# Two masked attentions with their experts: VectorE in program order, the side work cut finer and moved apart, one gate product per bank, GpSimd for the sums

## The chip, the cores and the metric

The kernel runs on one core of one Trainium2 chip. The metric is the device time of one execution in microseconds. The kernel before takes 2669.72 us, the median of three runs (2664.33 to 2672.69). One further execution was profiled; its own time is 2684.83 us.

The engines of the core are TensorE (PE; its weight loads are listed as PEld), VectorE (DVE), ScalarE (ACT), GpSimd (POOL) and SyncE (SP). Each takes its instructions from a queue of its own, in the order in which they were put there, and waits for the others by semaphores.

## The reference, cut to what matters

The reference is a stack of four transformer layers on x of 4 sequences x 512 positions x 128 features, all in fp32. Every layer is a "macaron": half a feed-forward part, an attention, half the same feed-forward part again, each on the layer-normed x. The change concerns layer 1, whose feed-forward part holds a masked attention of its own and a mixture of experts, and which the kernel therefore runs twice:

```python
q = (q_in @ Wq.T + bq).reshape(B, S, H, D)   # q_in: x, rotated in pairs (cosine and sine)
scores = jnp.einsum('bqhd,bkhd->bhqk', q, k) * scale        # 16 heads of 8, causal
attn = jax.nn.softmax(jnp.where(causal, scores, -jnp.inf), axis=-1)
x1 = _layer_norm(x + attn_out, ln1_w, ln1_b)
gates = jax.nn.softmax(x1 @ gate_w.T + gate_b, axis=-1)     # 8 experts
_, top_idx = jax.lax.top_k(gates, 2)
expert_outputs = jnp.einsum('bsd,efd->bsef', x1, expert_w) + expert_b
moe_out = jnp.sum(sel * top_gates[..., None], axis=2)       # the two chosen ones
return _layer_norm(x1 + moe_out, ln2_w, ln2_b)
```

The kernel multiplies all eight experts and gives the six that were not chosen a gate of zero.

## The kernel before, in words

**Tiles.** A sequence of 512 positions is four tiles of 128. Positions lie on the partitions in `x` and `y` (128 x 16 tiles x 128 features), features lie on the partitions in `yT`.

**The masked attention** is `dense_attention` (L820), called by `l1_ffn` (L999) with `masked=True`, once as "l1f" and once as "l1g". It has 16 units, 4 sequences b times 4 head groups j, and each unit has four steps n, one for every tile of keys. A step has two halves. In a half, TensorE multiplies two blocks of scores by keys (`pk_at`, for the step itself) and two blocks of scores by queries (`pq_at`, for the step five later, `LEAD`). VectorE takes the maxima of the latter (`maxima`, L856: one instruction at L866 that adds the mask and reduces, into `nm`), ScalarE takes the exponentials of the former into `PT` (L894), GpSimd zeroes the triangle above the diagonal (the causal select, L897), and TensorE multiplies the weights of the step before with the values into `po_at` (`with_values`, L902). At the start of a unit the maxima are transposed and added to the queries (`qx`, L876); at its end the sums are transposed and divided (L939, L940).

**The PSUM banks** of this stage are three for `pk_at`, three for `pq_at` (tag "q"), one for `po_at` and one for the side work (tag "m"). The expert products take banks of tag "q".

**The side work.** The next sequence is prepared by a list of parts, each with a place relative to the first step of that sequence (`prepare`, L1007: norm, scale, transposes, rotation, queries, keys with their masked copies, values). A place of -17.5 is the second half of the 18th step before. When a sequence has finished its attention, `l1_experts` (L1056) puts its rest into a chain: `spare(gap, part, products)` appends a part that runs `gap` ticks after the one before, and `tick` (L307), called once in every half step, runs what is due. Of the parts that put products on TensorE (`products` true, the default) one at most runs in a tick. The chain, with its gaps:

```python
spare(2, statistics_of_y, False); spare(4, lambda: affine(1), False); spare(4, lambda: turn(b))
spare(2, gates); spare(2, choice, False); spare(3, turn_gates); spare(2, biases)
for t in range(TB): spare(2, lambda t=t: both(t))
spare(1, statistics_of_y, False); spare(4, lambda: affine(2), False); spare(2, residual, False)
leave_normed(b, spare, 2)     # statistics of x 1 tick later, scale 1, transposes 2
```

The statistics of `y` and of `x` are four pairs of instructions (L242, L245) and a root, whose power runs on GpSimd (L214, L215). `affine` scales with four ScalarE instructions (L279) and multiplies and adds on GpSimd (L1069, L1070). `residual` adds `y` to `x` on GpSimd (L1140), and `leave_normed` (L314) then norms the new `x` for the next stage (statistics, scale L257, transposes). `both(t)` multiplies one tile with all eight experts into two banks and adds the eight results, each times its gate, to `y` with eight VectorE instructions (`sum_up`, L1117), every one reading what the one before wrote. The last sequence, b = 3, does all this after the attention, and its elementwise work on VectorE.

**The order of the queues.** TensorE's instructions are kept in program order by `mm_in_order`, ScalarE's by `by_order` within the attention. VectorE's and GpSimd's instructions are put into their queues by the scheduler of the tile framework, in the order in which its own model of the run finds them ready.

## Time and profile before

| what | us |
|---|---|
| median of three runs | 2669.72 |
| the profiled execution, its own time | 2684.83 |
| its span, from the first to the last instruction | 2683.0 |
| first masked attention, starts of units 0 to 15 | 383.7 to 644.8 |
| second masked attention, starts of units 0 to 15 | 833.3 to 1091.7 |
| a causal select on GpSimd (L897), mean | 0.410 |
| an addition of 128x512 on GpSimd (L1070), mean | 1.27 |
| an addition of 128x128 on GpSimd (L1275), mean | 0.454 |
| one expert's gate product and sum on VectorE (L1117), mean | 0.348 |
| a 128x512 product out of PSUM on VectorE (L1025), mean | 0.687 |

The page of the profile gives busy times of the engines, the chain of work that ended last, and groups of instructions by line. PE's busy time includes the modelled ends of its pipelined products, so a busy PE may still be a waiting one; the length of a unit says more. The granted clock is TensorE's, as a share of its full speed. In a row of a group or a timeline, "out<-in" names the tiles, and what stands in brackets or after the bar is the idle time of the engine just before it and what released it. In the timeline a row may merge several instructions (x8).

### The profile page before, as it was taken

How to read it: one execution, taken by the hardware profiler on the slowest of the kernel's cores; microseconds unless marked ns; L12 is line 12 of the kernel's file. 1: busy time of each engine (PE TensorE's matmuls, PEld its weight loads, DVE VectorE, ACT ScalarE, POOL GpSimd, SP SyncE). 2: the span in 40 equal slices, each digit the busy share in tenths (PEclk: the TensorE clock that was granted, in tenths of full speed). 3: DMA queues.
4: the chain of work that ended last, by engine and by line, in shares of the span. 5: the costliest groups of instructions: out<-in, count | busy, mean ns of one | idle time of the engine just before them, and what ended most of it. 6: DMA issues, size and time to landing. Idle time of an engine off the chain costs nothing.

```text
span 2683.0 us, 50819 instructions
## 1 busy us (share of the span) xinstructions
PE 2274.4 (85%) x19070; PEld 1288.0 (48%) x19070; DVE 1776.3 (66%) x4790; ACT 1306.2 (49%) x3159; POOL 951.7 (35%) x1532
## 2 busy tenths in 40 slices
PE   6578589988679989988787778998899998799988
PEld 2255244443344434477567645555433333555555
DVE  3745667775676777565554488777567775877774
ACT  3056125443333544343443357776525554677773
POOL 2023023232232233214331377766310001876761
PEclk8789799998889999789778879999989999899998
DMA  3052000000000000246145701010000000110100
GB/s 146 8 175 73 0 1 2 1 1 1 1 1 1 1 5 1 84 146 216 32 139 160 246 23 23 21 23 19 1 1 1 1 1 9 27 23 19 23 21 13
DMA packets 40142, 113.21 MB, mean 42 GB/s; under 512 B 7064, under 2 KB 16536, under 8 KB 39384
## 3 DMA queue, kind: packets, MB, share of 16 engines
q1 hardware_dynamic: 36520, 100.94, 11.8%
q0 software_dynamic: 2944, 6.04, 1.1%
q8 instruction: 151, 2.47, 0.4%
q10 hardware_dynamic: 432, 2.98, 0.3%
q14 instruction: 95, 0.78, 0.1%
HBM read 79.78 MB, written 15.47 MB: 35 GB/s over the span
## 4 chain that ended last, share of the span: by engine, by line
PE 56%; DVE 21%; ACT 8%; POOL 8%; issue 5%; DMA 1%; another core or an unknown queue 0%; POOLq 0%; DVEq 0%; SPq 0%; ACTq 0%
PE pk_at L185 10%; PE po_at L185 6%; PE pa L185 4%; PE pq_at L185 4%; PE pag L185 4%; PE po L185 3%; ACT s L1737 3%; PE pg L185 2%; PE pe L185 2%; PE p_qk L185 2%; DVE t L1794 2%; DVE t L1791 2%; PE pz L185 2%; PE idle L185 2%; PE pt L182 2%
## 5 line engine op out<-in xcount | busy, mean ns | idle before, releaser
L894 ACT ACTIVATE PT<-pk_at 128x512 f32<-128x512 f32 (+3 forms) x768 | 335.3, 488 | 401.2 <-PE pq_at L185 254.0
L185 PE MATMUL pk_at<-qx,km 32*128 32x512 f32 (+3 forms) x1536 | 401.4, 555 | 5.9 <-ACT PT L894 2.7
L866 DVE CUSTOM_DVE_ANT_0 s<-pq_at,cst 128x384 f32<-128x384 f32 (+3 forms) x512 | 249.9, 488 | 99.0 <-PE pq_at L185 44.8
L185 PE MATMUL pq_at<-km,qT 32*128 32x128 f32 (+3 forms) x1024 | 275.8, 504 | 18.3 <-DVE nm L866 14.4
L1737 ACT ACTIVATE s<-s,nm,rn 128x128 f32<-128x128 f32 x512 | 245.5, 482 | 3.2 <-DVE nm L1849 3.0
L897 POOL TENSOR_SCALAR_AFFINE_SELECT PT<-PT 128x256 f32<-128x256 f32 x256 | 104.5, 410 | 381.7 <-ACT PT L894 381.6
L185 PEld LDWEIGHTS pk_at<-qx,km 32*128 32x128 f32 x1536 | 147.1, 190 | 154.3 <-issue 93.5
L185 PE MATMUL po_at<-PT,vh 128*32 128x128 f32 (+3 forms) x2432 | 205.6, 395 | 8.7 <-POOL PT L897 6.9
L868 DVE TENSOR_REDUCE nm<-pq_at 128x1 f32<-128x512 f32 x256 | 165.4, 685 | 55.3 <-PE pq_at L185 53.8
L1798 POOL TENSOR_TENSOR t<-t,t 128x1024 f32<-128x1024 f32 x64 | 151.2, 2362 | 109.7 <-DVE t L1794 105.1
L215 POOL TENSOR_TENSOR ln_r<-ir,minus_half 128x4 f32<-128x4 f32 x60 | 62.0, 1034 | 351.5 <-DVE ir L214 349.5
L185 PE MATMUL pq_at<-km,t 32*128 32x512 f32 x512 | 170.9, 661 | 0.7 <-DVE nm L868 0.4
L185 PE MATMUL p_qk<-w,hT 128*128 128x512 f32 x256 | 142.4, 684 | 15.6 <-DVE t L1794 9.6
L1861 POOL TENSOR_TENSOR s<-s,sm 128x1024 f32<-128x1024 f32 x64 | 121.3, 1896 | 52.1 <-DVE sm L1860 44.1
L185 PEld LDWEIGHTS po_at<-PT,vh 128*32 128x32 f32 x2432 | 54.4, 109 | 174.4 <-issue 128.5
L182 PE MATMUL pt<-ident,s 128*128 128x128 f32 x640 | 94.0, 295 | 48.5 <-POOL s L1861 32.0
L185 PEld LDWEIGHTS pq_at<-km,qT 32*128 32x128 f32 x1024 | 110.6, 191 | 48.9 <-DVE nm L866 28.9
L1419 POOL DMA_INDIRECT xg<-yd,come x60 | 57.5, 958 | 180.3 <-PE pt_x L182 72.3
L289 ACT COPY yT<-pt_y 128x512 f32<-128x512 f32 x56 | 32.7, 584 | 180.0 <-PE pt_y L182 179.5
L1737 ACT ACTIVATE sq<-p_qk 128x1024 f32<-128x1024 f32 x64 | 65.5, 1023 | 109.8 <-PE p_qk L185 61.6
L182 PEld LDWEIGHTS pt<-ident,s 128*128 128x128 f32 x640 | 79.0, 151 | 81.1 <-POOL s L1861 44.2
L1791 DVE TENSOR_TENSOR t<-p_qk,w 128x1024 f32<-128x1024 f32 x64 | 78.3, 1223 | 58.5 <-ACT sq L1737 53.0
(457 smaller groups left out, 5374.7 us busy)
## 6 DMA issues: line engine op xcount, KB each, us to landing
wf<-in_w2f_dram SPq DMA_DIRECT2D x45, 836.0 KB
vb<-v SPq DMA_DIRECT2D x112, 128.0 KB
w<-in_w2f_dram SPq DMA_DIRECT2D x15, 836.0 KB
skew<-qe SPq DMA_DIRECT2D x16, 512.0 KB
rel<-skew SPq DMA_DIRECT2D x64, 128.0 KB
od<-o SPq DMA_DIRECT2D x60, 64.0 KB
w<-in_w_dram SPq DMA_DIRECT2D x1, 3200.0 KB
w<-in_w_dram SPq DMA_DIRECT2D x12, 173.0 KB
```

Source lines behind the costliest of these rows:

```text
L182: return nc.tensor.transpose(dst, src, ident[: src.shape[0], : src.shape[0]])
L185: tc.keep_in_program_order(nc.tensor.matmul(dst, lhsT=lhsT, rhs=rhs, start=start, stop=stop))
L215: nc.gpsimd.tensor_tensor(dst, v, minus_half[:, :n], ALU.pow)
L866: nc.vector.tensor_tensor_reduce(s[:, :nk], pq[:, :nk], causal[:, S - nk :], 1.0, -BIG, ALU.add, ALU.max, to)
L868: nc.vector.tensor_reduce(to, pq, AX.X, ALU.max)
L894: by_order(nc.scalar.activation(PT[:, i, q0:], pk[:, q0:], AF.Exp, scale=SC8))
L897: nc.gpsimd.affine_select(d, d, pattern=[[0, 2], [1, P]], base=0, channel_multiplier=-1, compare_op=ALU.is_ge, fill=0.0)
L1419: nc.gpsimd.indirect_dma_start(xT[s], None, yds[k][:, :], bass.IndirectOffsetOnAxis(ap=come[:, i : i + 1], axis=0))
L1737: tc.keep_in_program_order(nc.scalar.activation(*args, **kw))
L1791: nc.vector.tensor_mul(by_head(t1), by_head(p3), over(tab[:, 0]))
L1798: nc.gpsimd.tensor_add(t1, t1, t2)
L1861: nc.gpsimd.tensor_mul(s, s, bcast(sm, P))
```

## The change

1. **VectorE in program order.** Every VectorE instruction now goes through a small wrapper that keeps it in program order while a flag is set. The flag is set in a masked attention from step 0 to its end. (The diff replaces `nc.vector` by `vector` everywhere; those lines are left out here.)
2. **Finer parts, further apart.** For the sequences 0 to 2 the chain of `l1_experts` is written anew. Statistics come in two halves, the means, the scaling and the affine steps in parts of their own, the choice of experts in four parts, and the gaps are larger. In `prepare`, for the sequences 1 to 3, the statistics are halved, the cosines and the output bias become parts of their own ahead of the rotation, and the masked copies of the keys come two at a time. The copy of the keys `kT` now shares the buffer of `qin`.
3. **One gate product per bank.** `gated` multiplies one tile with four experts into one bank, and one VectorE instruction multiplies that bank with the four gates into a tile `by_act` of 128 x 4 x 128, of which there are three buffers.
4. **GpSimd sums.** `summed` adds the two halves of a tile, 128x512, then 128x256, then 128x128, and adds the result to `y`, four GpSimd instructions.

Sequence 3 keeps the chain of before. Counted in ticks from the start of a chain, its parts lie as follows:

| part | before | after, sequence 0 | after, 1 and 2 | after, 1 in the second attention |
|---|---|---|---|---|
| statistics of y | 2 | 1, 2 | 1, 2 | 1, 2 |
| gate logits | 12 | 12 | 12 | 12 |
| expert tiles | 21, 23, 25, 27 | 21 to 35, a bank every 2 | 20 to 27, a bank each | 19 to 22, a tile each |
| residual | 34 | 46 | 38 | 32 |
| statistics of x | 35 | 49, 50 | 41, 42 | 34, 35 |
| scale, transposes | 36, 38 | 52, 54 | 44, 46 | 37, 39 |

```diff
+    class InOrder:
+        def __getattr__(self, name):
+            op = getattr(nc.vector, name)
+            def issue(*args, **kw):
+                i = op(*args, **kw)
+                if ordered["dve"]:
+                    tc.keep_in_program_order(i)
+                return i
+            return issue
+    vector = InOrder()
...
+    def statistics_in_parts(src, b):
...
+            for t in (2 * i, 2 * i + 1):
+                vector.bn_stats(st[:, t, :], src[:, b * TB + t, :])
+                vector.bn_aggr(mv[:, t, :], st[:, t, :])
+            if i:
+                inverse_root(keep, r, mv[:, :, 1], "ir4", ALU.add, 1e-5, nc.gpsimd)
...
+        if pinned == "parts":
+            spare(start, halves[0], False)
+            spare(1, halves[1], False)
+            spare(2, scale, False)
...
         for n in range(-LEAD, n_steps + 5):
+            ordered["dve"] = masked and n >= 0
...
                 def rotate():
-                    nc.vector.tensor_mul(seq["in"], pw, ST)
-                    nc.gpsimd.tensor_add(yb, yb, rows(VEC(vec, "1f_bo"), TB))
-                    nc.gpsimd.tensor_mul(t2, yT[:, b, :], CT)
+                    vector.tensor_mul(t2, pw, ST)
                     vector.tensor_add(seq["in"], seq["in"], t2)
...
+                        (-19, norm), (-18.5, norm_more), (-17, scale), (-15.5, features), (-13.5, cosines), (-12.5, biased),
+                        (-11.5, rotate), (-9.5, queries), (-7.5, keys), (-6.5, lambda: mark((0, 1))),
+                        (-6, lambda: mark((2, 3))), (-5.5, last),
...
+        def gated(t, half):
+            pe = two_banks("pe1")[0] if "d" in psum["bufs"] else bank("e" if "e" in psum["bufs"] else "q", "pe1")
+            mm_in_order(pe, yT[:, b, ts(t, P)], ew[:, ts(half, 512)])
+            st["by", t, half] = sb.tile([P, 4, D], F32, tag="by_act", name="by_act", bufs=3)
+            vector.tensor_mul(
+                st["by", t, half], pe.rearrange("p (e d) -> p e d", d=D), bcast(st["g"][:, t, 4 * half : 4 * half + 4], D)
+            )
+        def summed(t):
+            v, w = st.pop(("by", t, 0)), st.pop(("by", t, 1))
+            yt = y[:, b * TB + t, :]
+            nc.gpsimd.tensor_add(v, v, w)
+            nc.gpsimd.tensor_add(v[:, 0:2, :], v[:, 0:2, :], v[:, 2:4, :])
+            nc.gpsimd.tensor_add(v[:, 0, :], v[:, 0, :], v[:, 1, :])
+            nc.gpsimd.tensor_add(yt, yt, v[:, 0, :])
...
+        next_part = 0 if routed and b == 1 else 1
+        if b < B - 1:
+            normed_in_parts(1, 1)
+            spare(3, lambda: turn(b))
+            spare(2, gates)
+            for f, gap in ((grow, 1), (share, 1), (best, next_part), (two_best, 1)):
+                spare(gap, f, False)
+            spare(1, turn_gates)
+            spare(2, biases)
+            for t in range(TB):
+                for half in range(2):
+                    spare((next_part if half else 1) if b else 2, lambda t=t, half=half: gated(t, half), False)
+                    if t and half == 0:
+                        spare(0, lambda t=t: summed(t - 1), False)
+            spare(1, lambda: summed(TB - 1), False)
+            normed_in_parts(2, 2 + next_part)
+            spare(1, residual, False)
+            leave_normed(b, spare, 2, "parts", 2 + next_part)
+            return
```

`normed_in_parts(n, gap)` places a norm of y in the chain: the two halves of the statistics, the means on GpSimd, the scaling on ScalarE in two halves, the multiplication and the addition of the affine step on GpSimd, at the gaps gap, 1, 1, 2, 1, 0 and 1.

## The prediction

> **What bounds the kernel now.** I read the page first (busy shares, then the shares of the chain that ended last), then a table of engine busy time with one row per unit of the two masked attentions, then the timeline and the chain of waits inside the worst units.
>
> ```profile
> span 2683.0 us, 50819 instructions
> PE 2274.4 (85%) x19070; PEld 1288.0 (48%) x19070; DVE 1776.3 (66%) x4790; ACT 1306.2 (49%) x3159; POOL 951.7 (35%) x1532
> ...
> PE 56%; DVE 21%; ACT 8%; POOL 8%; issue 5%; DMA 1%; another core or an unknown queue 0%; POOLq 0%; DVEq 0%; SPq 0%; ACTq 0%
> ```
>
> TensorE leads over the whole span, but that is an average. The change touches only the two masked attentions. Each has 16 units (4 sequences, 4 head groups), and a unit begins with its addition into `qx` (L876). The starts, read from the timeline, run from 383.7 to 644.8 us (units 0 to 14 of the first) and from 833.3 to 1091.7 us (the second). Rows for units 3, 8, 10 and 14 of the first; the columns are window, length, busy time of PE, PEld, DVE, ACT and POOL, granted clock, DMA:
>
> ```profile
> 424.70:436.90 12.20, 12.11 (x124) 6.23 (x124) 8.92 (x35) 6.59 (x17) 3.25 (x8) 1.00 0.01 2
> 500.60:519.50 18.90, 18.70 (x148) 8.60 (x152) 14.62 (x53) 7.52 (x19) 4.46 (x9) 1.00 0.01 1
> 542.30:567.80 25.50, 19.69 (x150) 9.21 (x150) 15.27 (x67) 10.69 (x26) 9.57 (x15) 0.87 0.00 1
> 621.10:644.80 23.70, 19.66 (x134) 8.17 (x136) 12.83 (x50) 9.79 (x26) 10.39 (x15) 0.71 0.00 1
> sum 261.10, PE 242.31 PEld 109.56 DVE 186.40 ACT 119.91 POOL 81.67; mean PE 16.15 PEld 7.30 DVE 12.43 ACT 7.99 POOL 5.44
> ```
>
> Unit 3 has no side work: 12.2 us is what a unit costs by itself. Unit 8 carries 6.44 us of side products on TensorE (two expert tiles, biases, transposes) and takes 18.9: **0.3 us over** 12.2 + 6.44. Unit 10 carries 4.43 us (the timeline has keys 1.13, transposes 1.12, gate logits 1.03, values 1.16) and takes 25.5: **8.9 us over**, at a clock of 0.87. I worked this for every unit. By the busy tables of the side tiles these products sum to 48.6 us in the first attention and 49.1 in the second, so the floors are 15 x 12.2 + 48.6 = 231.6 and 232.1 us, against 261.1 and 258.4. **55.8 us** in all lie above the floors: 35.7 in units 10 and 14 (8.9, 8.7, 8.8, 9.3), 7.8 in unit 5 (5.1, 2.7), 10.7 in units 9 and 13, 1.6 elsewhere. The chain of waits of unit 10, in order of time, says why:
>
> ```profile
> 543.19 1.53 ACT y L279 x4
> 544.80 1.28 POOL y L1069
> 546.15 1.28 POOL y L1070
> 547.51 1.28 POOL x L1140
> 548.81 0.49 DVE ln_st L242 x2
> ...
> 551.00 1.05 POOL ln_r L215
> 552.07 0.78 DVE y L257 x2
> 552.85 0.60 DVE s L866
> 553.51 1.64 PE pq_at L185 x2
> ```
>
> and VectorE's own timeline:
>
> ```profile
> 544.90 0.08 DVE L866 DVE_READ_ACCUMULATOR2_ANT nm<- 128x1 f32 x1
> 548.81 0.49 DVE L242 BATCH_NORM_STATS2 ln_st<-x 128x6 f32<-128x128 f32 x2 [3.82 <-POOL x L1140]
> ```
>
> A statistics instruction that needs GpSimd's residual sits in VectorE's queue ahead of maxima whose scores are ready. VectorE idles 3.82 us, then 1.16 for GpSimd's power; TensorE runs out of score banks (it waits 1.93 and 2.38 us for `nm`) and then runs slower. Unit 5 of the first attention shows another form: eight statistics in one clump, four of them a later sequence's, which the program has some ten steps on. VectorE's queue is not in program order.
>
> **The change, part by part.** *VectorE in program order, parts further apart.* By the tick counts, the residual was tick 34 of a sequence's chain and the statistics tick 35; they become 46 and 49 (sequence 0), 38 and 41 (1 and 2), 32 and 34 (sequence 1 of the second attention). A tick is half a step, 12.2 / 8 = 1.5 us bare, so the residual gets about 3 to 5 us instead of 1.5, and it needs up to 3 x 1.27 of GpSimd. The cause of units 10 and 14 should go. I leave 2 us in each, since the affine still fills GpSimd there (in unit 14 `po_at` itself waited 1.58 + 0.95 us for a causal select): 35.7 - 8 = **27.7**. Of unit 5 I take two thirds (the clump is split and put back in its place), **5.2**; of units 9 and 13 half, **5.3**. Bounds: nothing, and all 55.8. No instruction is added by the order. What is late next in these units is TensorE itself.
>
> *One gate product per bank.* 24 tiles (three sequences, two attentions) lose eight L1117 of 0.35 us, 2.78, and gain two 128x512 products out of PSUM; L1025, of that size and source, takes 0.686, so 1.37. VectorE gets 1.41 x 24 = 34 us free, which is **not on the path**: the expert units 8 and 12 are only 0.3 and 1.7 (0.9 and 1.7) over their floors, so at most 4.6 us. TensorE's own two products a tile stay. I take nothing.
>
> *GpSimd sums.* Four additions a tile: 128x512 1.27 (L1070), twice 128x128 at 0.454 (L1275), 128x256 between these, by columns 0.73: 2.91 us a tile, 70 us in all. The causal selects (0.41, two a step) queue behind them, and `po_at` waits for those. In two half steps with a tile (2 x 1.53 + 2 x 1.12 = 5.3 us) GpSimd has 2.91 + 0.82 = 3.7, so it keeps up, but single selects come late. Bounds a tile: nothing, and 1.6 us, TensorE's longest wait for a select in the first attention. I take 0.3, near the lower end since the sum falls between selects: **-7**; ends 0 and -38.
>
> *A new wait.* `by_act` has three buffers, and the second product of a tile writes the first buffer of the tile before, so VectorE waits there for that tile's last addition, with the maxima behind it. Sequence 0 has 5.3 us between tiles, enough. For sequences 1 and 2 (12 such places) a sum begun at its tick ends after 2.91 + 0.41 = 3.3 us, a half step with one product is 2.65: 0 to 0.7 late, or 1.2 with both selects ahead. I take 0.25: **-3**; ends 0 and -14.
>
> [...] VectorE's instructions that read SBUF only are stretched by GpSimd, those out of PSUM not. Minimum, median and maximum, in ns:
>
> ```profile
> L214 DVE TENSOR_SCALAR ir<-ln_mv x48: 151/170/1279, 9.2 to 2270.1; 128x4 f32<-128x4 f32 x48
> L371 DVE TENSOR_TENSOR oh<-g,fm x16: 182/187/940, 484.1 to 1159.0; 128x32 f32<-128x32 f32 x16
> L1117 DVE SCALAR_TENSOR_TENSOR y<-pe,g,y x240: 300/351/353, 508.8 to 1173.9; 128x128 f32<-128x128 f32 x120
> ```
>
> The 1.28 us one began at 626.64, with a GpSimd addition that began at 626.63. The new products and the maxima read PSUM. Some ten small instructions may meet the new sums at up to 1.1 us; most of that is covered by VectorE's idle time. I take **-2**; ends 0 and -10. [...]
>
> *The tail.* Sequence 2's chain is 46 ticks to its last transpose instead of 38, so eight ticks of it move behind the attention. In the next stage TensorE already waits 5.40 us for this chain's L257 (at 685.75). I take 2 us each: **-4**; ends 0 and -10. Splitting keys, cosines and statistics moves instructions without adding any, but for 0.24 of GpSimd a norm. On SP's queue the store of y that a logits step issues in the second attention moves from tick 39 to 55, 40 and 47; the gathers need sequences 0 and 1, and for 1 it is one tick.
>
> Sum: 27.7 + 5.2 + 5.3 - 7 - 3 - 2 - 4 = **22.2 us** faster. The profiled execution took 2684.8 us (span 2683.0 and 1.8 around it), 15 more than the median 2669.7. I take the difference from the median: **2647 us**.
>
> **Rivals.** (A) The forecast, 2647, own range 2632 to 2662.
> (B) *Full cure:* the order also clears units 5, 9 and 13, and the sums fit between selects: 55.8 less 8 to 12 of costs is 46, so 2624. For it: units 1 to 4, with side work well spread, are at most 0.3 us over their floors. Against: GpSimd is fullest where the stalls are.
> (C) *The stall only moves:* VectorE now waits in strict order for GpSimd's sums and roots, and gives back what the residual cost: 38 less 36, so 2668. For it: every wait of the worst units ends on GpSimd. Against: the distances are doubled or tripled.
> (D) *Slower: GpSimd becomes the bound of the expert tiles.* Place: the select behind a sum. Price: 1.6 us x 24 = 38 and the buffer wait 14, against 38 cured; with 4 of tail it is 18 slower, 2688. It decides from about 1.2 us a tile on. For it: 2.91 us of GpSimd in a half step of 2.65, and in the second attention, sequence 1, a whole tile every half step. Against: units with 9 to 10 us of GpSimd stall by VectorE first.
>
> **Chances.** A 0.57, B 0.15, C 0.11, D 0.17. Faster by over 0.3% (8 us, about what a measurement can tell from no change) 0.72, within 0.11, slower 0.17. The range 2616 to 2684 leaves out the ends of B and D.
>
> **What would show it.** Right: units 10 and 14 near 15 to 19 us at a clock of 1.00; no `ln_st` wait for `x` L1140 above 0.5 us; 48 products out of PSUM near 0.69; POOL some 70 us busier; L1117 down to the last sequence's 48. Wrong: `po_at` waiting for the select over 1 us a tile (D), VectorE waiting for `by_act` or `ln_r` by several us (C). If units 8 and 12 fall below 18 us, the product was worth more than I gave it.

## The result, and the profile after

The kernel after takes 2685.16 us, the median of four runs (2678.21 to 2689.87), beside 2670.95 us for the kernel before in the same comparison: a ratio of 1.0056, with a 95% interval of 1.0036 to 1.0075. The forecast was 2647, a ratio of 0.9915. Two further comparisons on other chips (below) give 1.0007 (0.9992 to 1.0022) and 1.0026 (1.0009 to 1.0042). So the change is worth nothing to half a per cent of loss, where 0.8% of gain was forecast. The kernel before takes 2671 to 2687 us by chip; times are therefore compared within one batch only.

The page of the kernel after: its instructions by engine, and the shares of the chain that ended last.

```profile
PE 2272.7 (85%) x19070; PEld 1289.5 (48%) x19070; DVE 1753.4 (66%) x4637; ACT 1304.1 (49%) x3159; POOL 1022.4 (38%) x1637
...
PE 54%; DVE 21%; POOL 9%; ACT 8%; issue 5%; DMA 3%; SPq 0%; POOLq 0%; DVEq 0%; ACTq 0%
```

The parts went in at their forecast prices: GpSimd is 70.7 us busier (forecast 70), VectorE has 153 instructions fewer. The instructions of the new tile, with their count and their least, median and longest duration in ns:

```profile
L184 DVE TENSOR_TENSOR by_act<-pe,g x48: 681/691/693, 510.1 to 1142.5; 128x512 f32<-128x512 f32 x48
L1230 POOL TENSOR_TENSOR by_act<-by_act x24: 1262/1272/1282, 515.0 to 1143.2; 128x512 f32<-128x512 f32 x24
```

(Every VectorE instruction of the kernel after is recorded at L184, the helper's line; matmuls are at L200, transposes at L197.)

Now the units of the first attention, as in the prediction. An attention's units are counted from 0, and the floor of a unit is the prediction's: 12.2 us and the busy time of its side products. Rows of the kernel after for units 7, 10, 11 and 14: window, length, busy time of PE, PEld, DVE, ACT and POOL, granted clock, DMA.

```profile
482.60:501.20 18.60, 16.04 (x136) 7.96 (x136) 13.50 (x63) 7.19 (x19) 4.52 (x10) 0.82 0.00 1
...
539.20:556.90 17.70, 15.92 (x140) 7.38 (x140) 12.41 (x47) 8.85 (x21) 9.37 (x18) 1.00 0.00 1
556.90:578.30 21.40, 18.20 (x148) 8.09 (x148) 14.43 (x62) 9.10 (x25) 7.07 (x11) 0.84 0.00 1
617.10:636.90 19.80, 17.72 (x141) 7.83 (x140) 10.85 (x46) 8.81 (x25) 9.05 (x16) 0.83 0.00 1
```

Unit 10 went from 25.5 us to 17.7, at a clock of 1.00: cured. Unit 14 went from 23.7 to 19.8. But unit 7 went from 13.9 to 18.6 and unit 11 from 13.5 to 21.4, both at a lower clock, and VectorE is busy 4 us longer in each. The rows of units 7 and 11 of the kernel before:

```profile
486.70:500.60 13.90, 13.67 (x128) 6.27 (x128) 9.53 (x41) 6.92 (x18) 3.30 (x8) 0.88 0.01 2
...
567.80:581.30 13.50, 13.36 (x140) 6.74 (x140) 10.08 (x42) 7.59 (x19) 3.31 (x8) 1.00 0.00 1
```

By stretches of the span, in three profiles of each kernel on three chips (us; an attention is from the start of its unit 0 to that of its unit 15; what is behind the second reaches to the first scores of layer 2's attention):

| stretch | before | after | difference of the means |
|---|---|---|---|
| first attention | 261.1, 258.5, 261.1 | 252.8, 248.9, 255.3 | -7.9 |
| behind it | 188.5, 194.5, 188.5 | 196.4, 197.9, 204.1 | +9.0 |
| second attention | 258.4, 258.4, 258.4 | 256.7, 256.8, 256.8 | -1.6 |
| behind it | 178.3, 177.2, 172.6 | 182.4, 182.5, 177.0 | +4.6 |
| the rest, which no edit touches | 1413.0, 1407.3, 1405.1 | 1404.1, 1410.9, 1395.8 | -4.9 |

The attentions gain 9.5 us and the stretches behind them lose 13.6. The rest differs by 8 to 15 us between profiles of one kernel. The profiled execution of the kernel before was 14 us above its median; beside that kernel's third profile, 8 us of it lie in the rest and 6 behind the second attention. So this table gives +4 us; the first comparison's 14 is not seen in full in any profile.

The same windows, split into the time in which TensorE was idle and the time in which it was busy (difference of the means of the three profiles, in us), with the mean granted clock:

| stretch | idle | busy | clock before | clock after |
|---|---|---|---|---|
| first attention | -3.6 | -4.3 | 0.93 | 0.94 |
| behind it | +1.5 | +7.5 | 0.87 | 0.81 |
| second attention | -5.5 | +3.9 | 0.95 | 0.91 |
| behind it | +1.9 | +2.7 | 0.87 | 0.85 |

The products of the four stretches are the same in both kernels; a dozen of some 2000 in an attention lie ahead of the start of unit 15 in the kernel after, and behind it in the kernel before, so the sums are safer than the single rows. By the sums TensorE waits 5.7 us less, and is busy 9.7 us longer with the same products, at a lower clock. The rows of the second attention, before and after (each repeats within 0.1 us in all three profiles):

```profile
833.30:1091.70 258.40, 240.32 (x1964) 110.56 (x1966) 184.90 (x716) 118.22 (x297) 77.21 (x156) 0.95 0.01 3
```

```profile
833.30:1090.00 256.70, 244.19 (x1976) 114.85 (x1976) 178.83 (x676) 118.17 (x299) 99.64 (x190) 0.91 0.01 3
```

### The profile page after: what moved, and what is told of

Read it like the earlier page. It is cut to its first block, busy times and chain, and to the rows that moved or that the text cites. A ratio compares the mean times of both kernels' runs of the same rounds, so it can differ in the third digit from the quotient of the medians.

```text
span 2676.5 us, 50723 instructions
## 1 busy us (share of the span) xinstructions
PE 2272.7 (85%) x19070; PEld 1289.5 (48%) x19070; DVE 1753.4 (66%) x4637; ACT 1304.1 (49%) x3159; POOL 1022.4 (38%) x1637
## 4 chain that ended last, share of the span: by engine, by line
PE 54%; DVE 21%; POOL 9%; ACT 8%; issue 5%; DMA 3%; SPq 0%; POOLq 0%; DVEq 0%; ACTq 0%
PE pk_at L200 11%; PE po_at L200 6%; DVE t L184 4%; PE pag L200 4%; PE pa L200 3%; PE pq_at L200 3%; PE po L200 3%; ACT s L1877 2%; PE p_qk L200 2%; PE pe L200 2%; PE idle L200 2%; PE pz L200 2%; DVE s L184 2%; PE pt L197 2%; DVE y L184 2%
## 5 line engine op out<-in xcount | busy, mean ns | idle before, releaser
L200 PE MATMUL pk_at<-qx,km 32*128 32x512 f32 (+3 forms) x1536 | 405.2, 566 | 4.1 <-DVE qx L184 1.4
L184 DVE CUSTOM_DVE_ANT_0 s<-pq_at,cst 128x384 f32<-128x384 f32 (+3 forms) x512 | 249.9, 488 | 116.1 <-PE pq_at L200 58.5
L200 PE MATMUL pq_at<-km,qT 32*128 32x128 f32 (+3 forms) x1024 | 268.6, 514 | 7.3 <-DVE nm L184 6.3
L200 PEld LDWEIGHTS pk_at<-qx,km 32*128 32x128 f32 x1536 | 149.5, 195 | 153.6 <-issue 91.6
L200 PE MATMUL po_at<-PT,vh 128*32 128x128 f32 (+3 forms) x2432 | 209.2, 397 | 11.3 <-POOL PT L937 11.2
L184 DVE TENSOR_REDUCE nm<-pq_at 128x1 f32<-128x512 f32 x256 | 165.2, 684 | 54.0 <-PE pq_at L200 52.9
L184 DVE TENSOR_TENSOR t<-p_qk,w 128x512 f32<-128x512 f32 (+1 forms) x192 | 155.2, 861 | 64.7 <-ACT sq L1877 61.1
L200 PE MATMUL pq_at<-km,t 32*128 32x512 f32 x512 | 169.4, 652 | 0.6 <-DVE nm L184 0.4
L200 PE MATMUL p_qk<-w,hT 128*128 128x512 f32 x256 | 142.6, 685 | 15.1 <-DVE t L184 9.2
L200 PEld LDWEIGHTS po_at<-PT,vh 128*32 128x32 f32 x2432 | 54.3, 111 | 184.3 <-issue 129.6
L197 PE MATMUL pt<-ident,s 128*128 128x128 f32 x640 | 92.3, 291 | 50.2 <-POOL s L2001 32.4
L200 PEld LDWEIGHTS pq_at<-km,qT 32*128 32x128 f32 x1024 | 109.6, 195 | 28.1 <-DVE nm L184 19.9
L197 PEld LDWEIGHTS pt<-ident,s 128*128 128x128 f32 x640 | 77.5, 149 | 82.3 <-POOL s L2001 45.0
```

Of the source, the lines that this page charges most:

```text
L184: i = op(*args, **kw)
L197: return nc.tensor.transpose(dst, src, ident[: src.shape[0], : src.shape[0]])
L200: tc.keep_in_program_order(nc.tensor.matmul(dst, lhsT=lhsT, rhs=rhs, start=start, stop=stop))
```

## What stalls in the kernel after

**Unit 7: VectorE's queue is full.** VectorE's timeline of the kernel after, start, duration, operation; only rows with an idle time in brackets at their end waited:

```profile
493.77 0.19 DVE L184 TENSOR_TENSOR oh<-g,fm 128x32 f32<-128x32 f32 x1
...
494.89 0.19 DVE L184 TENSOR_TENSOR g<-g,oh 128x32 f32<-128x32 f32 x1
495.00 0.25 DVE L184 RECIPROCAL rec<-pt_at 128x16 f32<-128x16 f32 x1
495.28 0.29 DVE L184 TENSOR_TENSOR ao<-pt_at,rec 128x128 f32<-128x128 f32 x1
```

and TensorE's, in the same place:

```profile
495.72 1.01 PE L197 MATMUL pt_g<-ident,g 128*8 128x128 f32 x4 [1.81 <-DVE ao L184]
```

From 488.0 to 497.3 VectorE's timeline has no idle row. In these 9 us lie the unit's wide maxima, the share, the best and the two best experts (16 small instructions of about 0.2 us, whose starts are 0.22 us apart), and the statistics of a later sequence's `x`. The turned gates `pt_g` stand one half step behind the last part of the choice, in TensorE's program order, and TensorE waits 1.81 us. The row names `ao`, not the gates `g`, which were done at 495.08. `ao` is the division at the end of the unit before. It reads `pt_at`, which lies in the one bank of the side work (tag "m") that `pt_g` needs next. `pt_at` was there from 491.3 on, but in program order the division stands behind the choice and ended at 495.57. So the choice holds TensorE up twice: by the gates, and for some 0.5 us more by the bank.

What follows costs more. The granted clock falls 0.6 us into this wait. The rows of the 3.4 us up to the fall, and of the 13.7 us from it on:

```profile
491.10:494.50 3.40, 2.06 (x18) 0.84 (x16) 2.98 (x16) 1.20 (x4) 0.81 (x2) 1.00 0.01 2
494.50:508.20 13.70, 12.48 (x88) 6.54 (x88) 8.22 (x35) 3.69 (x10) 2.89 (x6) 0.50 0.00 1
```

In the first, TensorE is idle 1.3 us: 0.75 for an earlier maximum (`nm`, at 492.75) and the beginning of the wait for `ao`. In the second the granted clock is 0.50 throughout, although TensorE is busy 12.48 us of 13.70.

**Unit 11: GpSimd's queue is in the wrong order.** GpSimd's timeline of the kernel after, and then the row of TensorE that waits:

```profile
562.21 1.27 POOL L1257 TENSOR_TENSOR y<-y,vec 128x512 f32<-128x512 f32 x1 [0.85 <-ACT y L1250]
563.55 1.28 POOL L1258 TENSOR_TENSOR y<-y,vec 128x512 f32<-128x512 f32 x1
564.91 1.32 POOL L1261 TENSOR_TENSOR x<-x,y 128x512 f32<-128x512 f32 x1
566.19 0.81 POOL L937 TENSOR_SCALAR_AFFINE_SELECT PT<-PT 128x256 f32<-128x256 f32 x2
```

```profile
566.65 1.92 PE L200 MATMUL po_at<-PT,vh 128*32 128x512 f32 x4 [1.97 <-POOL PT L937]
```

Program order was given to VectorE only. The scheduler still put multiplication, addition and residual of sequence 0 back to back on GpSimd, 3.9 us, ahead of two causal selects that TensorE needs. In the first attention `po_at` waits four times for a select, 0.98 to 2.03 us, 6.2 in all, none of them in units 8 or 9 with their expert tiles.

## The experiments

The expectations name theories by letters: P, GpSimd's work holds selects back and the clock falls behind that; O, VectorE's order costs by itself; L, the loss lies in later stages; W, the new waits of units 7 and 11 give back the gain. Ratios are to the kernel before in the same batch, with 95% intervals.

**The two kernels again**, twice, on two other chips (no edit; e1 and e13 are before, e2 and e14 after).

> The kernel before, unchanged, run again: it shows how far two sets of runs of one program lie apart, and gives a second profile. Three theories stand. Theory P (placement of GpSimd's work and the clock): the change removes VectorE's stall of units 10 and 14, but GpSimd's affine, residual and sums now hold back single causal selects, TensorE idles 1 to 2 us there, its granted clock halves behind them, and the longer chain of sequence 2 slows the end of both attentions. Theory O (order): the strict order of VectorE's queue costs by itself. Theory L (later stages): the attentions are even or faster, and the 14 us come from stages that the change does not touch, which differ from run to run. Here P and O expect 2670 within 3 us and the first attention at 261 us from unit 0 to unit 15, the second at 258; L expects the later stages (from 1270 us on) to differ by 5 us or more between the two profiles of this kernel.

> The changed kernel, unchanged, run again. P and O expect 10 to 18 us slower than before, and the profile to repeat the attentions of the first one (252.8 and 256.7 us from unit 0 to unit 15, with half clock for some 37 us from unit 15 of the second attention on). L expects the attentions to repeat too, and the rest of the span to be different from the first profile by 5 us or more.

> The kernel before, unchanged, for its profile beside that of the kernel after on the same chip. Ratio 1.000 within 0.15%.

> The kernel after, unchanged. If the first comparison holds, 1.004 to 1.007; if the repeat holds, 0.999 to 1.002. By the stages both kernels differ by -9 and -2 us in the attentions and +5 and +5 behind them, so I expect within 0.3%.

Before: 0.9990 (0.9976 to 1.0004) and 0.9993 (0.9980 to 1.0006). After: 1.0007 (0.9992 to 1.0022) and 1.0026 (1.0009 to 1.0042). P and O had expected 10 to 18 us of loss; e2 lies 2 us above e1 and e14 8 us above e13. The size of the loss differs by chip; that there is no gain doesn't. The profiles are those of the tables above: L fell, since the rest is shorter in the kernel after.

**After, with VectorE's queue left to the scheduler.**

```diff
-            ordered["dve"] = masked and n >= 0
+            ordered["dve"] = False
```

> The changed kernel with VectorE's queue left to the scheduler (the flag never set): finer parts, gate products and GpSimd sums stay. O expects it faster than the changed kernel by 8 us or more, at or below the kernel before. P expects it no faster than the changed kernel (0 to 15 us slower than it), since the parts' distances count only when VectorE's queue follows them, and GpSimd's work stays where it is.

2696.5 us, 1.0044 (1.0028 to 1.0059), 10 us above the copy of after in that batch; the attentions take 263.2 and 259.3 us. Its waits in the first attention (engine, tile, line, what it waited for, us in total, times, longest):

```profile
DVE ln_st L184 <- POOL y L1233: 5.1, 3, 2.4
DVE ln_st L184 <- POOL x L1261: 5.0, 2, 3.7
DVE y L184 <- POOL ln_r L230: 4.3, 3, 2.3
```

In the kernel after no such line is left. Without the order the scheduler draws the statistics forward again: those of `x` ahead of the residual, those of `y` ahead of GpSimd's sums (14.9 us of such waits in the second attention). But they stall other units now. Units 10 and 14 of both attentions took 99.6 us before and take 75.0 in the kernel after; here they take 77.1, while units 11 and 12 of the first attention take 22.3 and 23.9 us (13.5 and 20.5 before) and unit 9 stays at 23.0. So the new places of the parts relieve units 10 and 14 without the order; what the order adds is that these waits are gone in the other units too. O fell for the new chain.

**Before, with VectorE in program order and nothing else** (the helper of the change, and `ordered["dve"]` set in the masked attentions).

> The kernel before with VectorE in program order in the masked attentions and nothing else: old chain, old gaps, eight L1117 a tile, no GpSimd sums. O expects it 5 to 20 us slower than before. P expects units 10 and 14 still stalled (the statistics come one tick behind the residual, so VectorE waits for it in order), unit 5 of the first attention cured by 2 to 4 us, and the whole within 6 us of before.

2714.0 us, 1.0099 (1.0079 to 1.0119): 30 us slower, more than either side had expected. The attentions take 271.2 and 269.1 us. In the first attention TensorE now waits 3.3 and 2.5 us for `qx`, of which the kernel before has no such line, and the granted clock there is 0.89 (0.93 in the kernel before). Units 3, 4, 7 and 8, which had not stalled, lose 2.4 to 3.9 us each. Units 10 and 14 fall to 22.1 and 19.8 us there, and keep 25.0 and 24.2 in the second attention. That it is the lumps of the old chain (choice, four statistics, eight products) that hold the maxima up in program order is argued from these places, not shown.

**Before, with the statistics of the residual two half steps later and nothing else.**

```diff
-        leave_normed(b, spare, 2)
+        leave_normed(b, spare, 2, start=3 if b < 2 else 1)
```

> The kernel before with one gap changed: for sequences 0 and 1 the statistics of the residual are given three half steps behind it instead of one; no program order, no other part. If units 10 and 14 stall because the statistics stand one half step behind a residual that takes GpSimd up to 3 x 1.27 us, two more half steps (3 us) take most of the 35 us there away, and the time falls by 15 to 30 us to 2655 to 2669 without any of the rest. If it is the program order that makes distances hold (VectorE's queue is put together by the scheduler here, which may draw the statistics forward again), units 10 and 14 stay near 25 and 26 us and the time near 2684.

2687.4 us, 1.0052 (1.0039 to 1.0064); unit 10 takes 25.0 us, unit 14 takes 24.4. The attentions, 259.8 and 260.0 us, don't account for the 14 us of loss; the stretch behind the first takes 196.6. VectorE's timeline of this kernel has the old wait to the hundredth:

```profile
550.97 0.49 DVE L242 BATCH_NORM_STATS2 ln_st<-x 128x6 f32<-128x128 f32 x2 [3.82 <-POOL x L1140]
```

Distance for these statistics alone does nothing to the stall. Order alone costs 30 us and relieves units 10 and 14 in part. The new chain without order relieves them and stalls others (e3), and with order it stalls units 7 and 11.

**After, with the turned gates two half steps later.**

```diff
-            spare(1, turn_gates)
+            spare(3, turn_gates)
```

> The changed kernel with the transposes of the gates three ticks behind the last part of the choice instead of one (all later parts of a chain move by two ticks). The profile of the changed kernel shows TensorE waiting 1.8 us for the gates in units 7 and 11 and running at half clock behind that. If that new wait is what cost the gain (theory W), units 7 and 11 lose 2 to 4 us each in both attentions, 8 to 14 us in all, less up to 3 us for a longer tail: 0.2 to 0.5% faster than the changed kernel. If GpSimd's bursts are what cost it (theory P), unit 7 gets shorter by 2 us at most and unit 11 stays at 21 to 22 us, the whole within 4 us of the changed kernel.

2703.2 us, 1.0067 (1.0049 to 1.0085). The theory that the gates stand too near fell: TensorE's wait moved to the next scores, `pq_at` (2.21 us at 494.6, 4.38 at 572.9), and its waits for selects in the first attention grew from 6.2 us to 8.1. That with VectorE full someone waits wherever the gates stand is how I read these rows; it isn't tested further.

**After, with GpSimd in program order too** (the same helper around `nc.gpsimd` for the attentions and their chains), and that with the later gates.

> The changed kernel with GpSimd's instructions of the masked attentions in program order as well. In the changed kernel the scheduler put the multiplication, the addition and the residual of the affine back to back ahead of the causal selects, though the program places them a tick or more apart. P expects the TensorE waits for the select (1.9 us in unit 11, 1.3 and 0.8 in units 13 and 14, 2.1 in the second attention) to fall below 0.7, units 11, 13 and 14 to lose 2 to 4 us each, 8 to 16 us in all. W expects those units unchanged but for 1 us and the whole within 4 us of the changed kernel, or slower if strict order makes the selects wait for additions that are not ready.

> Both of the last two mends. If each names a cause of its own, the gains add: 15 to 28 us faster than the changed kernel and 10 to 25 faster than the kernel before. [...]

1.0003 (0.9988 to 1.0017) and 0.9991 (0.9977 to 1.0005). With GpSimd's order the attentions fall to 248.0 and 247.3 us, from 252.3 and 256.8 in the mean of after, unit 11 of the first from 21.4 to 17.8 and unit 14 from 19.8 to 14.9; TensorE's waits for selects fall from 6.2 us to 2.0 in the first. But the stretches behind take 204.6 and 188.3 us, from 199.5 and 180.6: nearly all of the gain is given back there. With the later gates too, the attentions take 251.3 and 249.0 us and the stretches 191.3 and 187.9; the 15 to 28 us that were expected if the two gains added did not come. No copy of after ran in this batch.

**After, with the old expert tiles** (one part a tile, eight L1117, no sums on GpSimd).

```diff
-                for half in range(2):
-                    spare((next_part if half else 1) if b else 2, lambda t=t, half=half: gated(t, half), False)
-                    if t and half == 0:
-                        spare(0, lambda t=t: summed(t - 1), False)
+                spare((1 + next_part) if b else 4, lambda t=t: both(t), False)
```

> The changed kernel with the expert tiles of before: both banks at once, eight L1117 of 0.35 us a tile on VectorE, in program order, no GpSimd sums; tiles at the same distances. It prices parts 3 and 4 of the change. The prediction took the products at no gain and the sums at a loss of 7 us: by it this kernel is 0 to 10 us faster than the changed one. If instead the short products are what makes program order bearable (a 2.8 us run of L1117 in order holds back four maxima), it is 8 to 30 us slower, with units 8, 9 and 12 above 21 us and VectorE named as releaser of the score products.

2703.0 us, 1.0076 (1.0057 to 1.0095); attentions 265.7 and 264.0. Under program order the short product and the sums together are worth some 20 us in the attentions. The residual of 128x512 (L1140 of the kernel before) took 1.26 us on GpSimd (6 instructions) and 0.68 on VectorE (2). No run here sets the sums alone on VectorE, behind the short product, so what that would give isn't shown.

**After, with six of eight experts left out of the sums.**

```diff
-            nc.gpsimd.tensor_add(v, v, w)
-            nc.gpsimd.tensor_add(v[:, 0:2, :], v[:, 0:2, :], v[:, 2:4, :])
-            nc.gpsimd.tensor_add(v[:, 0, :], v[:, 0, :], v[:, 1, :])
+            nc.gpsimd.tensor_add(v[:, 0, :], v[:, 0, :], w[:, 0, :])
```

> The kernel after, leaving out six of the eight expert products from the sums of sequences 0 to 2 (one addition of 128x128 and the one into y stay, two of the four additions of a tile go, about 2.0 us of GpSimd a tile, 48 us in all). My prediction took the sums at 7 us through late causal selects: then 3 to 9 us faster, 2677 to 2683. By the rival in which GpSimd bounds the expert tiles, 20 to 40 us faster, near 2655. If the selects are late only behind the affine and residual additions, as the traces of the kernel after look, no change within 3 us.

2669.3 us, 0.9986 (0.9975 to 0.9998). The attentions take 251.2 and 253.8 us, 4 less than the mean of after; behind them 198.0 and 178.7. Only the second is clear of scatter: 3 us below three profiles of after that agree within 0.1, while those of the first spread by 6. So two thirds of the sums' GpSimd time are worth 3 to 4 us in the attentions. No copy of after ran on this chip, so the whole time can't be set beside one.

**After, without the tie break of the choice.** Each maximum of eight gates is marked by comparison alone (2 instructions instead of 5).

```diff
         vector.tensor_tensor(oh, g, bcast(m, 8), ALU.is_equal)
+        if not ties:
+            return oh
```

> The kernel after, leaving out the tie break of the choice of two experts in sequences 0 to 2 (three of five 0.19 us instructions of each of the two maxima; equal gates would both be marked). If units 7 and 11 stall because VectorE, in program order, is full where the choice runs beside the wide maxima, the 1.1 us fewer of VectorE's time ahead of the turned gates take the 1.8 us wait of their transposes and the half clock behind it away: these units lose 3 to 7 us each, 8 to 15 us in all, 2671 to 2678. If the wait is for something else (GpSimd's work beside it, the exponentials), the time falls by 2 us at most, and units 7 and 11 stay near 18 and 21.5.

2670.8 us, 0.9990 (0.9978 to 1.0001). The attentions take 245.6 and 247.8 us, 15.7 less together than the mean of after. Unit 7 falls to 16.5 and 14.9, unit 11 to 19.2 and 20.8, where a 1.91 us wait for a select behind three additions on GpSimd is left. TensorE's wait for `ao` falls from 1.81 to 1.1 us in unit 7. That VectorE's small instructions of the choice stall these units is shown; that they are all is not. The stretches behind take 196.8 and 187.6 us, 4 more together than in the mean of after.

**Both causes away: GpSimd in order and the short choice.**

> The kernel after with GpSimd in program order in the masked attentions and without the tie break of the choice in sequences 0 to 2 (equal gates would both be marked). In the run with the short choice alone, unit 11 still lost 1.91 us waiting for a causal select behind three additions back to back on GpSimd, and units 7 and 11 kept 2 and 5 to 7 us above their floors. If these two are all, both units come to within 2 us of their floors, and the time is 5 to 12 us below the copy of after in this batch. If GpSimd's order only makes other instructions late, the gain over after stays at that of the short choice alone, 4 us or less.

2666.2 us, 0.9956 (0.9930 to 0.9983), 12.5 us below the copy of after. The twelve runs fall into two groups, five at 2644 to 2651 and seven at 2666 to 2678, hence the wide interval; the profile is of the upper group. Units 7 and 11 of its first attention:

```profile
487.20:504.50 17.30, 16.09 (x136) 8.26 (x136) 12.41 (x57) 7.19 (x19) 4.48 (x10) 0.86 0.01 1
563.50:580.00 16.50, 14.78 (x148) 7.56 (x148) 12.52 (x56) 9.14 (x25) 6.95 (x11) 1.00 0.01 1
```

Together units 7 and 11 of both attentions lie 10.5 us over their floors, from 23.1: the greater part of the new stall, though not within the 2 us a unit that I had expected. The attentions take 249.9 and 244.1 us, but the stretches behind them 203.0 and 185.9.

**The same without leaving anything out: GpSimd in order, the choice spread.**

```diff
-                        (-19, norm), (-18.5, norm_more), (-17, scale), (-15.5, features),
+                        (-21, norm), (-20.5, norm_more), (-17, scale), (-15.5, features),
...
-            for f, gap in ((grow, 1), (share, 1), (best, next_part), (two_best, 1)):
+            for f, gap in ((grow, 1), (share, 1), (best, next_part), (without_best, 1), (of_two, 1)):
...
-            normed_in_parts(2, 2 + next_part)
+            normed_in_parts(2, 2)
```

(`of_two` holds the last two of the eight instructions of `two_best`.)

> A version that computes all of it: the kernel after with GpSimd in program order, the last part of the choice in two half steps (its statistics after the experts one half step nearer, so that the chain is as long as it was), and the statistics of a later sequence's x two steps earlier, out of unit 7. If VectorE's fullness around the choice is the cause, units 7 and 11 fall by 2 to 5 us each, and the time is 4 to 10 us below the copy of after. If the wait only moves along the chain, as when the turned gates came later, within 3 us of it.

2668.4 us, 0.9982 (0.9966 to 0.9997), 10.3 us below the copy of after. The attentions take 246.5 and 248.1, and the stretches behind 202.4 and 187.8. Units 7 and 11 fall to 16.1 and 21.0 us (15.2 and 18.9 in the second attention), but unit 12 of the second attention, with its expert tiles, now takes 30.0 us, 23.2 in the kernel after: a part of the stall has moved once more.

**The stretch behind: sequence 2's chain shorter** (on the version with GpSimd's order and the later gates).

```diff
-        next_part = 0 if routed and b == 1 else 1
+        next_part = 0 if b == 2 or routed and b == 1 else 1
```

> The kernel after with GpSimd in program order, the turned gates three half steps behind the choice (as in the run that had both), and sequence 2's chain drawn together as sequence 1's is in the second attention (both products of a tile in one half step, the best in the share's), seven half steps shorter. If the 5 to 6 us behind the first attention and the 5 behind the second are lost because sequence 2's chain ends later, they come back: 2672 to 2677, faster than before by 0.3 to 0.5%. If the half clock of the throttle makes up that loss, or two products at once stall the units that carry them, the time stays at 2680 to 2688.

2688.3 us, 1.0052 (1.0038 to 1.0066); 196.9 and 194.5 us behind the attentions, where the version with the longer chain (e7) took 191.3 and 187.9. The theory that the mere length of this chain costs the time fell.

**The stretch behind: three operations of sequence 2 on VectorE.** Where GpSimd's additions of sequence 2 meet layer 1's other attention, VectorE's timeline of the kernel before and of the kernel after:

```profile
683.11 0.19 DVE L220 TENSOR_SCALAR ir<-rn 128x128 f32<-128x128 f32 x1
...
683.50 0.22 DVE L221 TENSOR_SCALAR ir<-ir 128x128 int32<-128x128 int32 x1
```

```profile
675.26 1.29 DVE L184 TENSOR_SCALAR ir<-rn 128x128 f32<-128x128 f32 x1
676.58 1.31 DVE L184 TENSOR_SCALAR ir<-ir 128x128 int32<-128x128 int32 x1
```

and what TensorE makes of it (where the kernel before waits 5.40 and 2.33 us for tiles `y`, at 685.75 and 689.38):

```profile
682.55 0.66 PE L197 MATMUL pt_1a<-ident,qkv 128*128 128x128 f32 x2 [8.08 <-DVE qkv L184]
```

In the kernel after three GpSimd instructions of 128x512 run from 675.19 to 679.14, and three VectorE instructions beside them, the third of 0.28 us before and 1.37 now, are stretched by 3.3 us in sum; in all three profiles of after, and in none of before.

```diff
+        late = {1: eng, 2: vector if b >= B - 2 else nc.gpsimd}
...
-            spare(0, lambda: nc.gpsimd.tensor_mul(yb, yb, rows(VEC(vec, f"ln{n}w"), TB)), False)
+            spare(0, lambda: late[n].tensor_mul(yb, yb, rows(VEC(vec, f"ln{n}w"), TB)), False)
```

> The kernel after, with the multiplication and addition behind the second norm and the residual of sequence 2 on VectorE (0.69 us each) instead of GpSimd (1.27). If the longer stretch behind the first attention comes from GpSimd's additions that stretch VectorE's instructions there from 0.2 to 1.3 us, TensorE's wait for the first transposes of layer 1's other attention falls from 8.1 us to 4 to 6, and the time by 2 to 6 us against the kernel after (ratio to before some 0.2% lower). If only the chain's length counts, the wait stays near 8 us and the time within 2 us.

> The version that computes all of it with the choice spread and GpSimd in order (0.9982 of before), and the same three operations of sequence 2 on VectorE. By the first theory 0.9960 to 0.9975 of before; by the other 0.998.

On after: 2685.6 us, 0.9994 (0.9980 to 1.0008). TensorE's wait fell from 8.1 us to 7.0 only, since VectorE now does the three operations itself; the stretch takes 192.2 us, within the spread of before. The ratio is lower than any of the three of after, but no copy of after ran in this batch, so this alone is inconclusive. On the spread version: 2673.6 us, **0.9946 (0.9930 to 0.9963)**, lower than either theory had it, and the fastest kernel of the study that computes everything. Its interval lies wholly below that of the spread version without the edit (e16, on another chip). Its attentions take 243.5 and 249.6 us, and the stretches behind them 188.4 and 192.0, after 202.4 and 187.8. In the first of these stretches TensorE is idle about as long, 44.0 us in e16 and 43.2 here; it is busy 158.4 and 145.2, at a clock of 0.79 and 0.86. So by these two profiles the three operations cost time there through the clock and hardly through longer waiting. In the second attention unit 12 still takes 31.4 us.

## Why the prediction was wrong, step by step

The sum took 26.2 us of gain for the attentions and 4 of loss behind them. By the stretches above they gained 9.5 and lost 13.6. Of the 26.3 us between the two, 16.7 are missing in the attentions and 9.6 behind them.

*Units 10 and 14* were 35.7 us over their floors and are now 12 (1.4, 1.4, 5.8, 3.4): 24 us, where 27.7 was taken. The cause named, statistics that stand ahead of a residual they need, was right. That VectorE's order is what relieves these units was not: with the new places alone they lose 22.5 us (e3). *Unit 5* went from 20.7 to 16.4 us in the first attention and from 18.3 to 19.1 in the second: 3.5, where 5.2 was taken. *Units 9 and 13* became 8.9 us shorter, some 3.4 of it by six expert products fewer (0.56 us each): 5.5, where 5.3 was taken.

*The expert product* was taken at nothing. Units 8 and 12 took 78.8 us and now take 84.0, with about 5.8 us more side products that lay in other units before: nothing gained there, as taken, and none of them fell below 18 us. But without the new tiles the attentions would be 20 us longer (e8). The line on L1117 had been costed against a queue that the scheduler orders. That in program order eight instructions in a chain hold up the maxima behind them fits these 20 us, but isn't shown apart from the rest of e8.

**The step that failed** is the sentence "What is late next in these units is TensorE itself", on which the sum took no cost from the parts that were moved. VectorE is late next, in units that had no stall: units 7 and 11 of both attentions went from 55.4 us to 79.6, from about their floors to some 23 us over them. The choice in four parts came to stand among the wide maxima of these units, and in program order neither can pass the other (e10); and on GpSimd, left to the scheduler, three additions of a norm stand ahead of selects (e6, e15). With both away 12.5 us come back (e15). I had read the stalls of the kernel before as belonging to the residual, and didn't add up VectorE's work in the units that the parts were moved to: unit 7 of after has 13.5 us of it, 9.5 before, in a unit that costs TensorE 12.2 and 2.1 of side products.

**What the sum left out** is the clock. The prediction saw it at 0.87 and 0.71 in units 10 and 14, and gave it no term: it counted waits only. The waits did become shorter, by 9.1 us in the attentions and 5.7 in all four stretches; but TensorE is busy 9.7 us longer with the same products.

*The tail* was taken at 4 us, with ends 0 and 10, and measures 13.6. Here the size failed: 3.4 us are longer waiting, near what was taken, and 10.2 are longer busy time. Shown in the traces are the three stretched instructions, and TensorE's wait of 1.95 us at the end of unit 15, where its transposes wait for a VectorE instruction that stands, in program order, behind products which wait for GpSimd's sums (0.60, 0.54 and 1.18 us). That last wait is gone in e11, with shorter sums: rival D's mechanism, at the end of the attention instead of in its expert units. But the stretch didn't become shorter by it (198.0 us), nor by the shorter chain (e12). The rows of the stretch behind the first attention, before and after:

```profile
644.80:833.30 188.50, 145.65 (x1082) 76.04 (x1084) 121.66 (x377) 64.16 (x135) 49.08 (x58) 0.88 0.00 1
```

```profile
636.90:833.30 196.40, 151.17 (x1074) 78.88 (x1076) 122.88 (x356) 64.35 (x135) 62.30 (x76) 0.83 0.00 1
```

TensorE is busy 5.5 us longer with no more matmuls, at a clock of 0.83 instead of 0.88, and idle 2.4 us longer. With the three operations on VectorE the clock comes back to 0.86 in one version (e18). Why it falls as it does, with about as much waiting in all, stays open; the kernel before has such a profile too (194.5 us at 0.84).

*The sums* (-7 taken) look about right: 3 to 4 us for two thirds of their time (e11). *The buffer wait* (-3 taken) is absent in the first attention and 1.6 us in the second; behind them VectorE waits 2.3 and 3.2 us for sums. *VectorE's stretched instructions* (-2 taken) were missed in their place: 3.3 us, in the tail.

*The rivals.* C, the stall only moves, comes nearest in time (2668 against a loss of 0 to 14 us), but not by its mechanism: VectorE in order waits in the first attention for TensorE alone, but for 1.5 us in rows named for a select, and no longer for a root or a residual, while TensorE still stalls. D, GpSimd bounding the expert tiles, did not come in its place: TensorE's waits for a select stand in other units, the one looked at behind additions of a norm, and units 8 and 9 of the first attention take 18.8 and 19.2 us, no longer than before. What happened is a case that the list lacked: the stall moves to the units that receive the moved work, and the waiting that is saved is spent again at a lower clock.

## What to carry to other kernels

When parts are moved apart and an engine is put in program order, add up that engine's work in the units that receive the parts, window by window, and not only in the units that are relieved. With one engine in order, look at what the scheduler does to the engines that share its path: with VectorE in order, GpSimd's additions stood ahead of selects. To put GpSimd in order too shortened the attentions by some 14 us, though not the whole kernel (e6). What is pushed behind a stage's end must be priced there. And split every stage into TensorE's idle and busy time, with the granted clock beside it: here the waits became shorter and the products longer.

## What the runs showed of the hardware that was not expected

TensorE's clock fell around short waits and stayed low for much longer. In unit 7 TensorE was idle for 1.3 of the 3.4 us up to 494.5; then the granted clock was half for 13.7 us, with TensorE busy for 12.48 of them. In unit 7 of the second attention it was idle for 1.7 of the 3.4 us up to 945.0; then the clock was half for 17.1 us:

```profile
941.60:945.00 3.40, 1.69 (x16) 0.62 (x14) 2.98 (x16) 0.87 (x3) 0.81 (x2) 1.00 0.02 5
945.00:962.10 17.10, 16.93 (x102) 7.59 (x106) 7.72 (x28) 4.77 (x12) 2.03 (x5) 0.50 0.00 0
```

All stretches at half clock in the changed stages of the kernel after are multiples of 3.4 us: 3.4, 6.8, 10.2, 13.7, 17.1 and, the longest, 37.5. So here the clock fell behind 3.4 us in which TensorE was idle for 1.3 and 1.7, and it stayed at half while TensorE was busy for 12.48 us of 13.7 and 16.93 of 17.1. What sets its fall and its return isn't shown.

Three VectorE instructions on SBUF alone, behind the first attention of the kernel after, each took about the whole time of the GpSimd instruction of 128x512 beside it: 1.29 us beside 1.27, 1.31 beside 1.26 and 1.37 beside 1.26, where the kernel before has 0.19, 0.22 and 0.28. The first two have one input. Not every such instruction is stretched: in unit 11 a sum and a reciprocal of gates (at 562.98 and 563.20) took 0.18 us each beside the multiplication that GpSimd ran from 562.21 to 563.48. Why some are stretched isn't shown.
